# Two pool stacks with waits by tile, and a first cross attention in two streams, three tiles ahead

## The chip, the cores and the metric

The kernel runs on one core of a Trainium2 chip. The metric is the device time of one execution in microseconds. Five engines work side by side, each through its own queue in order: TensorE (PE, with its weight loads shown as PEld), VectorE (DVE), ScalarE (ACT), GpSimd (POOL) and SyncE (SP), which here only issues transfers. They wait for each other through semaphores.

## The reference, cut to what matters

The input x has 16 rows of 128 tokens of 256 numbers; each row is one tile `x[t]` in SBUF. The network has four layers, and each layer is a cross attention to a context of the same size and then a feed-forward part.

- Layer 0: cross attention with 16 heads and quantised products, `h = layernorm(x); x += attend(h, ctx_t)`, which needs only tile t and its context. Then causal self-attention within the tile with 16 query heads and 4 key heads of 128, and a mixture of eight experts, of which two are combined per token (the kernel computes all eight and weights them).
- Layer 1: one-headed cross attention to the tile's context with a mask, then a gated feed-forward part whose three weight matrices are rounded to -1, 0 and 1 by the mean of their absolute values: `s = 1/mean|w|; w_q = clip(round(w*s), -1, 1)/s`. This rounding is part of the computation and is done in the kernel.
- Layer 2: cross attention with 16 heads to the tile's context, then a feed-forward part that picks 4 of 64 small experts.
- Layer 3: cross attention of every tile to the keys and values of all 16 tiles' contexts, then a mixture of ten experts.

Every tile passes the layers in turn; only layer 3's keys and values join the tiles, and those depend on the context alone.

## The kernel before

`run` works in three stages. `l0` (L561) is layer 0; `middle` (L862) is layers 1 and 2 with the keys and values of layer 3; `l3` (L883) is layer 3. Within a stage several streams of tiles stand at different points of the work. Each stream has its own SBUF pool, a pool of small tiles and a tag that names the PSUM banks it uses (`stream`, L116). The work of a tile is a Python generator cut into steps by `yield`, and `side_by_side` (L122) goes through the running generators step by step. A scheduler then orders the instructions of each engine; it may move an instruction ahead of its step, so the steps are only a guide. In `l3` alone the order is the written one.

Layer 0, per tile t:

- `l0_xattn` (L342), the cross attention, starts at step 4t and takes seven steps. Its heads come in four groups (`attention`, L249). Per group POOL spreads the keys (kx, L259), PE makes scores (L262), DVE takes the maximum and subtracts it (L264, L271), ACT the exponential (L272), PE transposes (L209), ACT copies (L225) and PE multiplies with the values (av, L278).
- `l0_keys` (L482) starts at step 4t+8: keys and values of the self-attention.
- `l0_group` (L504) starts at steps 4t+11 to 4t+14, once for each four query heads: projection q, rotation and norm (L464), transposes, scores (L518), softmax on DVE, ACT and POOL (L520 to L527), transposes, oT (L531), and output projection (oproj, L539).
- `l0_moe` (L545) starts at step 4t+17: routing, eight gate-and-up products (gu), and the down product (moe).

The eight PSUM banks of layer 0 are x, av, aq, a, as and ap with one buffer each and m with two. The query tiles of a group go through aq, the scores through as, and everything is transposed through a, so that the groups follow each other in a chain.

SBUF is one stack: a stage's pools are opened over those of the stage before, and every tile of a new pool waits until all of the old pool that it overlaps has been released. `middle` begins with `l1_ffn_weights` (L612). It loads the three raw matrices, sums their absolute values on DVE (L622), multiplies the sums with a matrix of ones on PE (L624), scales and clips on DVE (L631, L632) and converts on ACT (L633). Then come the other weights of the middle, in the order of SP's queue. The expert weights of layer 3 (pool w4) are loaded after the middle.

Of the kernel before, what the change touches and what calls it, by code (L numbers as in the profile page):

```python
# [40 lines left out]
class Net:  # L41
    def __init__(self, tc, pools, ins, out):
        self.tc, self.nc, self.i, self.out = tc, tc.nc, ins, out
        self.const, self.small = pools
        self.small0 = self.small
        self.ps = self.tag = None
        self.setup()
# [66 lines left out]

    @contextmanager
    def stream(self, name, bufs=2, small=3, tag=None):  # L116

        with (self.tc.tile_pool(name=name, bufs=bufs) as pool,
              self.tc.tile_pool(name=f"{name}_s", bufs=small) as sm):
            yield pool, sm, tag or name  # L120

    def side_by_side(self, starts):  # L122


        running, step = [], 0
        while running or any(k >= step for k in starts):
            running += [(st, make(self.enter(st))) for st, make in starts.get(step, ())]
            still = []
            for st, gen in running:
                self.enter(st)  # L130
                try:
                    next(gen)
                    still.append((st, gen))
                except StopIteration:
                    pass
            running, step = still, step + 1
# [12 lines left out]
    @contextmanager  # L149
    def psum(self, **bufs):  # L150

        with self.tc.tile_pool(name="psum", bufs=1, space=PSUM) as self.ps:
            self.bufs = bufs
            yield
            self.ps = None

    def bank(self, shape, tag, name, dtype=F32):
        return self.ps.tile(shape, dtype, name=name, tag=tag, bufs=self.bufs[tag])
# [90 lines left out]
    def attention(self, qT, kT, v, scale, pool, per_row=False):  # L249
# [4 lines left out]
        av = self.bank([P, NH, 17], "av", "av")  # L254

        def group(g):
            oc, hs = g // 2, slice(4 * (g % 2), 4 * (g % 2) + 4)
            kx = pool.tile([P, 4, P], F32, name="kx", tag="kx", bufs=2)
            nc.gpsimd.tensor_tensor(kx, kT[oc].unsqueeze(1).to_broadcast([P, 4, P]),  # L259
                                    self.hmask[:, hs].unsqueeze(2).to_broadcast([P, 4, P]), ALU.mult)  # L260
            ps = self.mm([P, 4, P], "scores")
            nc.tensor.matmul(ps, qT[:, oc, :], kx, start=True, stop=True)  # L262
            mx = self.s(4, "mx")
            nc.vector.tensor_reduce(mx, ps, AX.X, ALU.max, negate=per_row)  # L264
            p = pool.tile([P, 4, P], F32, name="p", tag="p", bufs=3 if per_row else 2)
            if per_row:
                nc.vector.tensor_scalar(mx, mx, scale, None, ALU.mult)  # L267
                for h in range(4):
                    nc.scalar.activation(p[:, h, :], ps[:, h, :], AF.Exp, bias=mx[:, h:h + 1], scale=scale)  # L269
            else:  # L270
                nc.vector.tensor_tensor(p, ps, mx.unsqueeze(2).to_broadcast([P, 4, P]), ALU.subtract)  # L271
                nc.scalar.activation(p, p, AF.Exp, scale=scale)  # L272
            return p

        def product(g, p):
            pT = self.transposed(p.rearrange("p h k -> p (h k)"), 4, pool, "pT", bufs=1 if per_row else 2)
            for h in range(4):
                nc.tensor.matmul(av[:, 4 * g + h, :], pT[:, h, :], v[:, 4 * g + h, :], start=True, stop=True)  # L278
# [52 lines left out]
    def l0_xattn_weights(self):  # L331
        w = {}
        with self.tc.tile_pool(name="l0x_q", bufs=1) as pool:
# [110 lines left out]
    def l0_ffn_weights(self, pool):  # L444
        nc, w = self.nc, {}
        w["q"] = self.load("L0_ffn_qT", [P, 2, 2048], "wa", "(c p) n -> p c n", p=P)
        w["kv"] = self.load("L0_ffn_kvT", [P, 2, 1024], "wc", "(c p) n -> p c n", p=P)
# [13 lines left out]
        w["moe"] = self.moe_weights("L0_ffn", 8)  # L461
# [94 lines left out]
    @contextmanager  # L556
    def l0_weights(self, pool):
        self.tag = "x"
        yield self.l0_xattn_weights(), self.l0_ffn_weights(pool)

    def l0(self):  # L561

        with self.tc.tile_pool(name="l0w", bufs=1) as wp, self.psum(x=1, av=1, aq=1, a=1, **{"as": 1}, ap=1, m=2), self.l0_weights(wp) as (wx, wf), (
                self.stream("x", bufs=1, small=2)) as sx, self.stream("a") as sa, self.stream("m", small=2) as sm:
            tiles = {}

            starts = {}
            for t in range(NT):
                starts.setdefault(4 * t, []).append((sx, lambda p, t=t: self.l0_xattn(t, wx, p)))
                starts.setdefault(4 * t + 8, []).append((sa, lambda p, t=t: self.l0_keys(t, wf, tiles, p)))  # L570
                for g in range(4):
                    starts.setdefault(4 * t + 11 + g, []).append(
                        (sa, lambda p, t=t, g=g: self.l0_group(t, g, wf, tiles, p)))
                starts.setdefault(4 * t + 17, []).append((sm, lambda p, t=t: self.l0_moe(t, wf, tiles, p)))
            self.side_by_side(starts)
        self.tag, self.small = None, self.small0
# [35 lines left out]
    def l1_ffn_weights(self):  # L612

        nc, W = self.nc, self.W1
        w = {"subln": self.rows("L1_ffn_subln_weight", "subln")}
        with self.tc.tile_pool(name="l1r", bufs=1) as pool:
            raw = [self.load("L1_ffn_gateT", [P, 2, W], "ra", "(c p) n -> p c n", p=P, pool=pool),
                   self.load("L1_ffn_upT", [P, 2, W], "rb", "(c p) n -> p c n", p=P, pool=pool),
                   self.load("L1_ffn_downT", [P, 8, D], "rc", "(c p) n -> p c n", p=P, pool=pool)]
            sums = self.s(3, "wsum")  # L620
            for j, r in enumerate(raw):
                nc.vector.tensor_reduce(sums[:, j:j + 1], r, AX.XY, ALU.add, apply_absolute_value=True)  # L622
            ps = self.mm([P, 3], "wtot")
            nc.tensor.matmul(ps, self.ones, sums, start=True, stop=True)  # L624
            mean = w["mean"] = self.w.tile([P, 3], F32, name="wmean", tag="wmean")
            nc.vector.tensor_scalar(mean, ps, 1.0 / (W * D), 1e-5, ALU.mult, ALU.max)
            r = self.s(3, "wr")
            nc.vector.reciprocal(r, mean)
            for j, (n, v) in enumerate(zip(("gate", "up", "down"), raw)):
                w[n] = self.w.tile(list(v.shape), BF16, name=f"tern{j}", tag=f"tern{j}")  # L630
                nc.vector.tensor_scalar(v, v, r[:, j:j + 1], 1.0, ALU.mult, ALU.min)  # L631
                nc.vector.tensor_scalar(v, v, -1.0, MAGIC, ALU.max, ALU.add)  # L632
                nc.scalar.activation(w[n], v, AF.Identity, bias=self.unmagic)  # L633
        return w
# [227 lines left out]
    def middle(self, w3):  # L862

        with (self.tc.tile_pool(name="w1", bufs=1) as self.w, self.psum(e=1, w=3, x=2, av=1, f=1)):
            self.tag = "e"
            w1f = self.l1_ffn_weights()
            w2x, w2f, w3k = self.l2_xattn_weights(), self.l2_ffn_weights(), self.l3_kv_weights()
            with (self.stream("f", bufs=1, small=2) as s2f, self.stream("x", bufs=1, small=2) as s2x,
                  self.stream("kv", bufs=1, small=2, tag="f") as s3, self.stream("f1", bufs=1, small=2, tag="e") as s1f,
                  self.stream("x1", bufs=1, small=2, tag="e") as s1x):  # L870
                starts = {}
                for t in range(NT):
                    for step, st, make in ((0, s1x, lambda p, t=t: self.l1_xattn(t, p)),
                                           (3, s1f, lambda p, t=t: self.l1_ffn(t, w1f, p)),
                                           (7, s2x, lambda p, t=t: self.l2_xattn(t, w2x, p)),
                                           (16, s2f, lambda p, t=t: self.l2_ffn(t, w2f, p)),
                                           (2, s3, lambda p, t=t: self.l3_keys(t, w3k, w3, p))):
                        starts.setdefault(4 * t + step, []).append((st, make))
                starts[4].append((s3, lambda p: self.l3_values(w3k, w3, p)))
                self.side_by_side(starts)  # L880
        self.tag, self.small = None, self.small0

    def l3(self, w3, moe_w):  # L883
# [13 lines left out]
        with (tc.tile_pool(name="l3x", bufs=2) as pool, tc.tile_pool(name="l3p", bufs=3) as pp,  # L897
              tc.tile_pool(name="l3t", bufs=LAG + 1) as tp, tc.tile_pool(name="l3m", bufs=1) as mp,
              tc.tile_pool(name="l3e", bufs=3) as ep):
# [282 lines left out]
    def run(self):  # L1182
        self.load_x()
        with self.tc.tile_pool(name="w0", bufs=1) as self.w:
            self.l0()
        with self.tc.tile_pool(name="w3", bufs=1) as self.w:
            w3 = self.l3_weights()
            self.middle(w3)
            with self.tc.tile_pool(name="w4", bufs=1) as self.w:
# [72 lines left out]
```

## Time and profile before

| what | value |
|---|---|
| median of three runs | 3008.33 us (3003.62 to 3014.27) |
| profiled execution, its own time | 3011.51 us |
| its span, first to last instruction | 3009.8 us |
| PE, DVE, ACT, POOL busy, whole span | 82%, 65%, 58%, 33% |
| layer 0 (first cross attention to last expert product) | 27 to 1154.6 us |
| a tile of layer 0 between 336 and 892 us | 61.8 us |
| layer 1's first readout and first gate product | 1182.1 and 1192.0 us |
| the middle's last output product ends | 1862.5 us |
| layer 3's first exponential | 1877.5 us |

All times within a trace count from the first instruction. A line of a timeline gives the start, the duration, the engine, the line of the kernel, the operation, output and inputs, and in brackets how long the engine was idle before it and what ended that. The profile of the stages gives busy time per engine in a window; as matmuls are pipelined and their ends modelled, busy PE is not always PE at its peak.

### The profile page before, as it was taken

How to read it: one execution, taken by the hardware profiler on the slowest of the kernel's cores; microseconds unless marked ns; L12 is line 12 of the kernel's file. 1: busy time of each engine (PE TensorE's matmuls, PEld its weight loads, DVE VectorE, ACT ScalarE, POOL GpSimd, SP SyncE). 2: the span in 40 equal slices, each digit the busy share in tenths (PEclk: the TensorE clock that was granted, in tenths of full speed). 3: DMA queues.
4: the chain of work that ended last, by engine and by line, in shares of the span. 5: the costliest groups of instructions: out<-in, count | busy, mean ns of one | idle time of the engine just before them, and what ended most of it. 6: DMA issues, size and time to landing. Idle time of an engine off the chain costs nothing. (4 is left out here: it accounts for less than half of the span.)

```text
span 3009.8 us, 41685 instructions
## 1 busy us (share of the span) xinstructions
PE 2460.5 (82%) x14066; PEld 1556.2 (52%) x14066; DVE 1956.3 (65%) x5041; ACT 1755.0 (58%) x4636; POOL 1000.7 (33%) x1587
## 2 busy tenths in 40 slices
PE   4789999999999875888888885777777777777778
PEld 2456666666666543456555653344444444444445
DVE  2455666666665434566666653887788787878784
ACT  1234444444444332555555541998888888888885
POOL 2344444444443322555555541111111111112111
PEclk9899999999999887999999997589899898989999
DMA  5000000000000003000000002876666666666673
GB/s 205 1 1 1 1 1 1 1 1 1 1 1 1 1 28 102 6 3 5 5 5 4 3 1 72 154 135 123 124 117 128 121 124 121 126 122 125 118 128 62
DMA packets 559830, 171.38 MB, mean 57 GB/s; under 512 B 538912, under 2 KB 555904, under 8 KB 558848
## 3 DMA queue, kind: packets, MB, share of 16 engines
q1 hardware_dynamic: 559616, 168.72, 27.8%
q8 instruction: 111, 1.82, 0.2%
q14 instruction: 103, 0.84, 0.1%
HBM read 32.37 MB, written 2.10 MB: 11 GB/s over the span
## 5 line engine op out<-in xcount | busy, mean ns | idle before, releaser
L938 ACT ACTIVATE p<-piece,nb,hs 128x512 int16<-128x512 f32 x1024 | 785.2, 791 | 27.4 <-issue 17.0
L922 DVE TENSOR_REDUCE nm<-piece 128x1 f32<-128x512 f32 x1024 | 652.1, 684 | 107.7 <-PE piece L916 99.8
L916 PE MATMUL piece<-kst,qT 128*128 128x512 bf16 x1024 | 366.5, 414 | 200.6 <-DVE ma L1099 89.6
L1100 POOL TENSOR_TENSOR act<-ma,mb 128x176 f32<-128x176 f32 x160 | 89.0, 558 | 765.1 <-DVE ma L1099 764.7
L233 PE MATMUL gu<-w_L_ffn_wgu,mhT 128*128 128x352 f32 x640 | 252.5, 523 | 11.6 <-ACT p L938 8.0
L225 ACT COPY pT<-tp 128x512 f32<-128x512 f32 (+1 forms) x208 | 116.6, 563 | 201.6 <-PE tp L209 200.1
L916 PEld LDWEIGHTS <-qT 128*128 128x128 bf16 x1024 | 77.4, 99 | 297.2 <-issue 168.8
L938 ACT ACTIVATION_READ_ACCUMULATOR p<-piece,nb,hs 128x1 f32 x1024 | 222.2, 217 | 0.0
L259 POOL TENSOR_TENSOR kx<-kT,hmask 128x512 f32<-128x512 f32 x128 | 132.8, 1043 | 190.4 <-PE scores L262 125.4
L264 DVE TENSOR_REDUCE mx<-scores 128x4 f32<-128x512 f32 x128 | 88.2, 689 | 161.3 <-PE scores L262 161.0
L233 PEld LDWEIGHTS gu<-w_L_ffn_wgu,mhT 128*128 128x128 f32 x640 | 122.7, 205 | 131.4 <-ACT p L938 83.5
L950 PEld LDWEIGHTS <-pT 128*128 128x128 f16 x4096 | 144.7, 99 | 82.6 <-issue 68.0
L278 PEld LDWEIGHTS av<-v,pT 128*128 128x128 f32 x1024 | 136.2, 201 | 78.2 <-ACT pT L225 66.6
L233 PE MATMUL gu<-w_L_ffn_wgu,hT 128*128 128x352 f32 x512 | 173.7, 461 | 2.1 <-DVE act L432 1.6
L524 ACT ACTIVATE s<-s,nb,qs 128x128 f32<-128x128 f32 x256 | 123.2, 482 | 87.2 <-DVE nb L522 87.2
L278 PE MATMUL av<-v,pT 128*128 128x17 f32 x1024 | 136.3, 265 | 41.0 <-ACT pT L225 41.0
L269 ACT ACTIVATE p<-scores,mx,qs 128x128 f32<-128x128 f32 x256 | 96.9, 459 | 118.8 <-DVE mx L267 111.0
L950 PE MATMUL av<-v_int,pT 128*128 128x16 bf16 x4096 | 143.7, 171 | 19.6 <-DVE o L1021 19.6
L262 PE MATMUL scores<-kx,qT 128*128 128x512 f32 x256 | 153.0, 682 | 2.3 <-ACT qT L225 1.8
L539 PE MATMUL oproj<-w_L_ffn_oT,oT 128*128 128x256 f32 x512 | 128.9, 396 | 3.7 <-ACT oT L533 3.6
L1119 PE MATMUL moe<-w_L_ffn_wd,aT 128*128 128x256 f32 x448 | 127.7, 434 | 3.6 <-ACT p L938 3.6
L233 PE MATMUL q<-w_L_ffn_qT,hT 128*128 128x512 f32 x256 | 127.9, 600 | 2.1 <-DVE rot L478 2.0
(362 smaller groups left out, 5305.7 us busy)
## 6 DMA issues: line engine op xcount, KB each, us to landing
pT<-p SPq DMA_TRANSPOSE x256, 4.3
w_L_ffn_wgu<-in_L_ffn_wgu SPq DMA_DIRECT2D x1, 3520.0 KB, 11.6
w_L_ffn_wgu<-in_L_ffn_wgu SPq DMA_DIRECT2D x1, 2816.0 KB, 12.7
x<-in_x SPq DMA_DIRECT2D x16, 128.0 KB, 4.5
ctxT<-in_ctxT SPq DMA_DIRECT2D x4, 512.0 KB, 5.2
w_L_ffn_qT<-in_L_ffn_qT SPq DMA_DIRECT2D x1, 2048.0 KB, 7.9
w_L_ffn_oT<-in_L_ffn_oT SPq DMA_DIRECT2D x1, 2048.0 KB, 15.6
ctx<-in_ctx SPq DMA_DIRECT2D x16, 128.0 KB, 2.0
```

What stands on the lines that cost most here:

```text
L225: nc.scalar.copy(out[:, j0:j0 + m, :], ps)
L233: self.nc.tensor.matmul(ps, a, b, start=(j == 0), stop=(j == n - 1))
L259: nc.gpsimd.tensor_tensor(kx, kT[oc].unsqueeze(1).to_broadcast([P, 4, P]), self.hmask[:, hs].unsqueeze(2).to_broadcast([P, 4, P]), ALU.mult)
L262: nc.tensor.matmul(ps, qT[:, oc, :], kx, start=True, stop=True)
L278: nc.tensor.matmul(av[:, 4 * g + h, :], pT[:, h, :], v[:, 4 * g + h, :], start=True, stop=True)
L524: nc.scalar.activation(s[:, j, :], s[:, j, :], AF.Exp, bias=nb[:, j:j + 1], scale=qs[:, j:j + 1], accum_out=z[:, j:j + 1])
L539: nc.tensor.matmul(proj, oT[:, j, :], w["o"][:, c, :], start=(c == 0), stop=(c == 15))
L916: nc.tensor.matmul(ps, qTs[t % 2][:, hd, :], kst[q // 2][:, hd // 2, 512 * (q % 2):512 * (q % 2) + 512], start=True, stop=True)
L922: nc.vector.tensor_reduce(st["nm", u][:, q:q + 1], st["s", u, q][0], AX.X, ALU.max, negate=True)
L938: nc.scalar.activation(p[:, 512 * q:512 * q + 512], ps, AF.Exp, bias=nb, scale=st["sq", t][:, hd:hd + 1], accum_out=st["z", t][:, hd, q:q ...
L950: nc.tensor.matmul(st["av", t][:, hd, :], pb[:, c, :], v[:, c, hd * 16:(hd + 1) * 16], start=(c == 0), stop=(c == NT - 1))
L1119: nc.tensor.matmul(ps, st["aT", k][:r, j, :], wd[:r, c, :], start=(c == 0), stop=(c == 13))
```

## The change

All SBUF and PSUM pools are now opened with waits by tile: a tile waits only for those old tiles whose bytes it takes. SBUF becomes two stacks, one from the left and one from the right end. On the left stand the weights and the stream of layer 0's self-attention, its expert weights and, from step 17, the expert stream; on the right stand the cross attention's weights and streams. The weights of layer 1 (`w1`) and the layer 1 streams of the middle follow on the right, and the weights of the middle (`w2`) and the layer 2 streams on the left.

Layer 0's cross attention runs in two streams at first. Tiles 1, 3 and 5 use a second stream `y`, with the banks of the expert stream (m0 for its products, m1 for av) and single buffers; tiles 0, 2 and 4 use stream `x`. Tile t starts at step 2t up to tile 5 and at 4(t-3) after that, so that from tile 6 on the cross attention is three tiles further ahead. Stream y is closed before the experts begin.

`l1_ffn_weights` becomes a generator, `prepare`, that starts at step 60 of layer 0, once the cross attention is over; it has two raw buffers instead of three, sums and converts one matrix after the other, and uses bank x. In the built program its DVE passes stand among the work of tiles 10 and 11. In layer 0's loads the keys' weights come before the query weights.

```diff
+    def pool(self, name, bufs, side="left"):
+        return self.tc.tile_pool(name=name, bufs=bufs, side=side, reuse_waits="tile")
...
-    def side_by_side(self, starts):
+    def side_by_side(self, starts, hooks={}):
         running, step = [], 0
         while running or any(k >= step for k in starts):
+            if step in hooks:
+                hooks[step]()
...
-        with self.tc.tile_pool(name="psum", bufs=1, space=PSUM) as self.ps:
+        with self.tc.tile_pool(name="psum", bufs=1, space=PSUM, reuse_waits="tile") as self.ps:
...
     def bank(self, shape, tag, name, dtype=F32):
+        if tag == "m":
+            self.turns += 1
+            tag = ("m0", "m1")[self.turns % 2]
...
-        av = self.bank([P, NH, 17], "av", "av")
+        twice = 1 if self.tag == "m0" else 2
+        av = self.bank([P, NH, 17], "m1" if self.tag == "m0" else "av", "av")
...
-            kx = pool.tile([P, 4, P], F32, name="kx", tag="kx", bufs=2)
+            kx = pool.tile([P, 4, P], F32, name="kx", tag="kx", bufs=twice)
...
+        w["kv"] = self.load("L0_ffn_kvT", [P, 2, 1024], "wc", "(c p) n -> p c n", p=P)
         w["q"] = self.load("L0_ffn_qT", [P, 2, 2048], "wa", "(c p) n -> p c n", p=P)
-        w["kv"] = self.load("L0_ffn_kvT", [P, 2, 1024], "wc", "(c p) n -> p c n", p=P)
...
+    def l0(self, late):
+        early = ExitStack()
         self.tag = "x"
+        with self.psum(x=1, av=1, aq=1, a=1, **{"as": 1}, ap=1, m0=1, m1=1):
+            self.w = early.enter_context(self.pool("wx", 1, "right"))
+            wx = self.l0_xattn_weights()
+            sx = early.enter_context(self.stream("x", bufs=1, small=2, side="right"))
+            with (self.pool("wa", 1) as self.w, self.stream("a") as sa, self.pool("wm", 1) as wm,
+                  ExitStack() as third):
+                wf = self.l0_ffn_weights(self.w)
+                self.w = wm
+                wf["moe"] = self.moe_weights("L0_ffn", 8)
+                self.tiles(wx, wf, sx, sa, early, late, third)
...
+    def tiles(self, wx, wf, sx, sa, early, late, third):
+        ahead, BEGIN = ExitStack(), 17
+        sy, sm = ahead.enter_context(self.stream("y", bufs=1, small=2, tag="m0", side="right")), []
+        def begin():
+            ahead.close()
+            sm.extend(third.enter_context(self.stream("m", small=2)))
+        hooks[BEGIN] = begin
+        def prepare(pool):
+            early.close()
+            self.w = late.enter_context(self.pool("w1", 1, "right"))
+            yield from self.l1_ffn_weights()
             for t in range(NT):
-                starts.setdefault(4 * t, []).append((sx, lambda p, t=t: self.l0_xattn(t, wx, p)))
+            other = t in (1, 3, 5)
+            step = 2 * t if t < 6 else 4 * (t - 3)
+            starts.setdefault(step, []).append((sy if other else sx, lambda p, t=t: self.l0_xattn(t, wx, p)))
...
+        starts.setdefault(4 * NT - 4, []).append((sa, prepare))
+        self.side_by_side(starts, hooks)
...
-            sums = self.s(3, "wsum")
-            for j, r in enumerate(raw):
-                nc.vector.tensor_reduce(sums[:, j:j + 1], r, AX.XY, ALU.add, apply_absolute_value=True)
+            for j, (n, shape) in enumerate(shapes.items()):
+                yield
+                if j == 2:
+                    raw[n] = self.load(f"L1_ffn_{n}T", shape, "raw0", "(c p) n -> p c n", p=P, pool=pool)
+                v, total, r = raw[n], self.s(1, "wsum"), self.s(1, "wr")
+                nc.vector.tensor_reduce(total, v, AX.XY, ALU.add, apply_absolute_value=True)
+                ps = self.bank([P, 1], "x", "wtot")
...
-        with (self.tc.tile_pool(name="w1", bufs=1) as self.w, self.psum(e=1, w=3, x=2, av=1, f=1)):
-            w1f = self.l1_ffn_weights()
+        w1f = self.w1f
+        with (self.psum(e=1, w=3, x=2, av=1, f=1), self.stream("x1", bufs=1, small=2, tag="e", side="right") as s1x,
+              self.stream("f1", bufs=1, small=2, tag="e", side="right") as s1f, self.pool("w2", 1) as self.w,
+              self.stream("kv", bufs=1, small=2, tag="f") as s3, self.stream("x", bufs=1, small=2) as s2x,
+              self.stream("f", bufs=1, small=2) as s2f):
...
-            with self.tc.tile_pool(name="w4", bufs=1) as self.w:
+            late.close()
+            with self.pool("w4", 1, "right") as self.w:
```

## The prediction

> **What bounds the kernel now.** I read first the busy time by stage, because the change touches only some stages. Columns: window, its length, then busy time (instructions) of PE, PEld, DVE, ACT and POOL, granted clock, DMA share, GB/s.
>
> ```profile
> 27.00:86.00 59.00, 35.88 (x100) 20.37 (x100) 19.16 (x52) 7.37 (x17) 19.83 (x36) 1.00 0.36 124
> 86.00:140.00 54.00, 39.99 (x138) 22.77 (x138) 22.65 (x54) 14.71 (x32) 20.25 (x30) 0.78 0.00 0
> 140.00:211.00 71.00, 59.91 (x272) 39.09 (x271) 36.85 (x86) 29.21 (x77) 33.44 (x46) 0.90 0.00 1
> ...
> 336.00:892.00 556.00, 524.23 (x2547) 359.74 (x2546) 342.55 (x918) 255.24 (x702) 255.03 (x363) 1.00 0.00 1
> ...
> 954.00:1017.00 63.00, 54.10 (x210) 35.02 (x209) 29.78 (x87) 23.91 (x68) 23.43 (x33) 0.86 0.00 1
> 1017.00:1075.00 58.00, 50.91 (x211) 32.80 (x210) 28.07 (x75) 23.45 (x67) 20.71 (x30) 0.97 0.00 1
> ...
> 1154.50:1192.00 37.50, 12.50 (x33) 5.81 (x33) 18.16 (x49) 8.84 (x11) 11.16 (x25) 0.61 0.56 174
> ...
> 1820.00:1863.00 43.00, 20.57 (x66) 13.93 (x66) 13.71 (x29) 3.91 (x7) 9.63 (x10) 0.72 0.00 0
> ```
>
> From 336 to 892 PE is busy 94%: nine tiles in 556 us, 61.8 us a tile, bound by PE. Only three places have slack: the ramp (27 to 211), the last tiles of layer 0, which have no cross attention beside them (954 to 1075), and the two seams (1154 to 1192, 1820 to 1863). At the first seam PE works 12.5 of 37.5 us. Its timeline says why:
>
> ```profile
> 1154.62 0.37 SPq L95 DMA_DIRECT2D w_L_xattn_Wq<-in_L_xattn_Wq  x1
> ...
> 1165.79 3.75 PE L233 MATMUL kv<-w_L_xattn_kvT,ctxT 128*128 128x512 f32 x4 [6.82 <-DMA w_L_xattn_oT<-in_L_xattn_oT]
> ...
> 1176.93 2.08 PE L233 MATMUL k<-w_L_xattn_Wkv,ctxT 128*128 128x256 f32 x4 [7.39 <-DMA w_L_xattn_Wkv<-in_L_xattn_Wkv]
> ...
> 1182.06 1.22 PE L607 MATMUL read<-ctx,pT 128*128 128x256 f32 x2 [0.35 <-ACT pT L225]
> ...
> 1191.95 1.06 PE L233 MATMUL gate<-tern,hT 128*128 128x512 bf16 x2
> ```
>
> The last expert product of layer 0 ends at 1154.59. Only then does the first weight of the middle leave SP's queue, since its pool waits for the whole of layer 0; PE waits for those bytes twice.
>
> Last, single rows of the ramp. The same two matmuls of 512 columns take 2.07 us there and 1.10 in a dense stage:
>
> ```profile
> 36.93 2.07 PE L262 MATMUL scores<-kx,qT 128*128 128x512 f32 x2 [0.46 <-ACT qT L225]
> ...
> 44.69 2.05 PE L262 MATMUL scores<-kx,qT 128*128 128x512 f32 x2
> ```
> ```profile
> 1800.38 1.10 PE L262 MATMUL scores<-kx,qT 128*128 128x512 f32 x2
> ```
>
> PE runs at half speed in the ramp (the clock column's 1.00 from 27 to 86 is not borne out by these durations, which decide).
>
> **Part 1: first seam, gain.** In the changed build the middle's weights take bytes 101,664 to 138,608 of a partition. Those held layer 0's attention stream (99,136 to 139,460), not the expert weights (from 139,488). The attention stream's last tile is read by the residual add that ends at 1120.5 and the normalisation that ends at 1121.8. Before, the loads took from 1154.6 to 1176.9, 22.3 us; begun at 1121.8 they land by 1144, ten microseconds before PE needs them. Layer 1's ternary weights are loaded and rounded earlier still, in layer 0. What remains after the last expert product, with the cold rows of the trace in the new PE order: transpose 0.5, key projection 2.1 beside the copy 0.4, scores 0.7, the four kv matmuls 3.7 (softmax, 1.2, lies under them), transpose and copy 0.8: the readout starts 7.9 us after the product, where it started 27.5 after (1182.06 less 1154.59). From there to the gate matmul 9.9 us stay. Gain 19.6, some 22 if PE stays at full speed, 16 if the loads are up to 4 us late. I take 20.
>
> Before the seam, in the last tile's experts, DVE's third sum over raw weights (2.28 us from 1136.87) keeps the next expert waiting until 1139.07 although its ACT result stood at 1137.34. That sum moves away: gain 1.7.
>
> **Part 2: second seam, next to nothing.** PE's order is unchanged there: layer 3's first transpose stands behind the last output matmul of the middle in both builds, and the chain before it (x add, routes, z, transposes, output) is untouched. The zeroing of the two query buffers on POOL (1.80 each) moves from ahead of a power that the last tile waits for (delayed from about 1822.6 to 1824.4, partly under DVE's routes) to the place after z, under 6 us of output matmuls. Gain 1 (0 to 2). Layer 3's expert weights may load sooner, but are first used some 30 units into layer 3.
>
> **Part 3: cross attention two tiles abreast, three ahead.** A tile of it costs PE 12.8 us: its rows between 700 and 762 sum to 15.1 of 69.2, scaled to the 58.5 us that PE was busy. Three tiles, 38 us, move from the steady stage into the ramp, where PE is idle 23, 14 and 11 us of the first three windows: 48. With everything hidden the ramp grows by nothing; with nothing hidden, by 38, or more with PE at half speed. In between stands a chain: one group of a tile takes 7.75 us (36.93 to 44.69), 5.1 of it PE. Two groups in the new order share PE: transposes 1.1, wait for the copy 1.3, products 1.9, scores 2.06, twice: 12.8 at half speed. At full speed 0.6, 1.3, 1.0, 1.1 makes 8.0 for two.
>
> Which of them is a matter of the clock. Row: PE's longest run in the old ramp is 3.8 us (products and scores), then 3.7 idle, and it stayed slow. Rule: the Trainium skill, "TensorE: Matmul & The Clock Gate", section "What's actually happening", has PE doubled in speed after a window of about 3.4 us sustained work, and halved after such a window idle. The new runs (products, scores, next transposes) are 5.1 us and the waits 1.3, so the rule says full speed after a round or two: the ramp then grows by about 6 us. By the old rows alone it grows by some 30: four rounds at 12.8 for 7.75 are 20, and another 9 or so until the third tile. I take 6, range -8 to 30.
>
> The same rule speaks against the other end. Layer 0's last tiles lose their cross attention: five tiles instead of two run without it. That should save 12.8 a tile, but the two that did took 63 and 58 us (the projections start at 954, 1017 and 1075), not 49: the chain of each group sets the pace, and PE falls idle long enough to slow down:
>
> ```profile
> 994.06 1.11 PE L209 MATMUL tp<-ident,s 128*128 128x128 f32 x4 [3.70 <-POOL s L527]
> ...
> 998.59 3.78 PE L539 MATMUL oproj<-w_L_ffn_oT,oT 128*128 128x256 f32 x8 [0.68 <-ACT oT L533]
> ```
>
> (Eight of those take 1.89 elsewhere.) Three more such tiles at 60.7 for 61.8 save 3; at 58, 11; at 63 they lose 4. I take 3.
>
> **Part 4: layer 1's weights inside layer 0, cost.** Three sums of 2.28, six passes of 1.2 to 1.3 (14.3 us of DVE) and three ACT passes of 2.0 now stand in the queues of tiles about 10 and 11, with softmax steps of a group behind them on both engines; PE waits for those. The passes had been on idle engines; the cover is DVE's idle half (28 of 58 us busy). One row warns:
>
> ```profile
> 1163.43 1.21 DVE L632 TENSOR_SCALAR w_L_ffn_downT<-w_L_ffn_downT 128x2048 f32<-128x2048 f32 x1
> ...
> 1163.57 1.48 POOL L178 TENSOR_TENSOR ln_r<-rp,mhalf 128x1 f32<-128x1 f32 x1
> ```
>
> POOL's power takes 0.55 elsewhere, so a DVE pass can hold POOL, which ends each group's softmax. The third load also waits until ACT has freed the first raw buffer (1 MB, 5 to 10 us to land), and DVE's queue waits with it. All twelve hidden costs 0; half of each in the way, 10. I take 4 (0 to 12). SP's added waits hold back nothing else in layer 0, which issues no other transfer then; two mask loads wait for POOL's casts of tiles 0 and 1, which also lie in layer 0, ahead of the middle's weights. At the start the expert weights (2.8 MB) now go before the keys' weights, about 10 us later for these; they are needed near 86, forty microseconds after.
>
> **Sum.** +6 - 3 + 4 - 1.7 - 20 - 1 = -15.7. On the span of 3009.8: 2994; the profiled run's time is 1.7 above its span, 2996, and stands 3.2 above the median of the runs: 3008.3 - 15.7 = 2992.6. I say 2993.
>
> **Rivals.** (a) The seam's gain stands and the rest nets to nothing or little: 2977 to 2999, likeliest. (b) The ramp and the weight passes eat it: ramp +15, passes +8, late tiles 0: 3008 - 20 - 2.7 + 23 = 3008. For it: PE's 94% means that moved work is not removed work. Within 0.3% of 3008.3 (9 us, about what a measurement of this kernel can tell from no change), 2999 to 3017. (c) Slower: PE stays at half speed through the two-stream ramp. Ramp +32, late tiles +4, passes +8, against 22.7: 3030. It decides once the ramp grows by more than about 31 with the other terms as taken. Against it: the 5.1 us runs. (d) More gain: the ramp runs dense enough to gain the half-speed stretches back (-8), late tiles at 58 (-11), seam 22: 2968. (e) The pools change nothing, because some tile of the middle still sits on late bytes: the seam stays, and +5 remains: 3013. The byte addresses speak against it; it is counted in (b).
>
> **Chances.** (a) 0.47, (b) with (e) 0.22, (c) 0.14, (d) 0.17. Faster 0.64, same 0.22, slower 0.14. The range reaches from (d)'s near half to past (b): 2966 to 3020; (a)'s own is 2977 to 2999.
>
> **What would show it.** Right: PE's gap after the last expert product under 3 us, the readout 6 to 9 us behind it; SP issuing the middle's weights some 30 us before that product; score pairs of 1.1 us by the third round of the ramp; the last five tiles of layer 0 near 60 us each. Wrong: score pairs still at 2.07 us beyond 80 us; POOL's softmax products delayed around the weight passes; layer 0 ending more than 20 us later than before.

## The result, and the profile after

The changed kernel takes 2985.96 us, median of five runs (2978.52 to 2997.94), beside 3008.33 for the kernel before: ratio 0.9927, 95% interval 0.9898 to 0.9956, 22.4 us less. Its profiled execution took 2981.85 us with a span of 2980.1, at a mean granted clock of 0.922. The profiled execution before shows 0.922 too, but has no clock record ahead of 91 us, and by its rows PE ran at half speed there from 27 us on; counted so, its mean is about 0.91 (an estimate). The two profiled executions lie 29.7 us apart, 7.3 more than the medians: one was 3.2 us slower than its kernel's median, the other 4.1 faster. The stages below add up to the 29.7.

The stages after, in the columns of the stage table of before (window, length, busy time and instructions of PE, PEld, DVE, ACT and POOL, granted clock, DMA share, GB/s):

```profile
27.00:86.00 59.00, 43.60 (x208) 27.97 (x207) 32.24 (x74) 15.65 (x34) 26.54 (x43) 0.86 0.36 130
86.00:140.00 54.00, 46.71 (x217) 30.31 (x218) 30.80 (x76) 19.07 (x43) 26.03 (x36) 0.87 0.00 1
140.00:211.00 71.00, 63.59 (x313) 42.94 (x312) 42.87 (x104) 31.79 (x82) 35.31 (x49) 0.93 0.00 1
338.50:892.00 553.50, 507.63 (x2368) 343.34 (x2367) 336.19 (x878) 247.89 (x672) 235.92 (x341) 0.98 0.02 8
962.50:1022.60 60.10, 51.41 (x207) 32.88 (x206) 27.47 (x76) 23.70 (x67) 20.42 (x29) 0.91 0.00 1
1022.60:1081.00 58.40, 51.32 (x213) 32.74 (x212) 29.00 (x79) 23.67 (x66) 21.16 (x31) 0.97 0.02 5
1158.80:1174.00 15.20, 7.75 (x31) 4.26 (x30) 7.86 (x30) 3.03 (x8) 7.23 (x14) 0.72 0.04 10
1795.00:1837.00 42.00, 21.13 (x66) 14.52 (x66) 12.04 (x27) 3.91 (x7) 9.60 (x10) 0.67 0.21 82
```

The first three windows hold more PE work than before (153.9 us for 135.8), as meant. In the fourth the granted clock is 0.98 where it was 1.00, and the layer is no shorter: its last expert product ends at 1158.8, before at 1154.6. The seam is another matter: 15.1 us from that product to the first gate product, where it was 37.4. Its timeline, SP's queue first, then PE:

```profile
1041.40 0.38 SPq L96 DMA_DIRECT2D w_L_xattn_qT<-in_L_xattn_qT  x1
...
1086.66 0.46 SPq L96 DMA_DIRECT2D w_L_xattn_Wq<-in_L_xattn_Wq  x1
...
1127.44 0.37 SPq L96 DMA_DIRECT2D w_L_xattn_Wkv<-in_L_xattn_Wkv  x1
```
```profile
1153.80 5.02 PE L243 MATMUL moe<-w_L_ffn_wd,actT 128*128 128x256 f32 x22 [0.56 <-DVE actT L237]
1158.65 0.38 PE L219 MATMUL tp<-ident,ln_h 128*128 128x128 f32 x2
1158.87 1.03 PE L243 MATMUL k<-w_L_xattn_Wkv,ctxT 128*128 128x256 f32 x4
...
1162.58 0.70 PE L644 MATMUL read<-ctx,pT 128*128 128x256 f32 x2 [0.35 <-ACT pT L235]
1169.48 1.01 PE L827 MATMUL htp<-identb,parts 128*128 128x128 bf16 x8 [6.21 <-DVE qs L251]
...
1173.89 0.63 PE L243 MATMUL gate<-tern_gate,hT 128*128 128x512 bf16 x1 [0.22 <-issue]
```

The weights leave 117 to 31 us ahead of the product's end and PE goes on without a gap, the key projection at full speed (1.03 us; cold 2.08). The readout stands 3.8 us behind the product, before 27.5.

In the ramp the pairs of score matmuls reach 1.10 us in the third round of the changed kernel, where the first five of the kernel before, up to 80.8 us, took 2.05 to 2.07:

```profile
34.84 1.38 PE L273 MATMUL scores<-kx,qT 128*128 128x512 f32 x2 [0.46 <-ACT qT L235]
37.11 2.04 PE L273 MATMUL scores<-kx,qT 128*128 128x512 f32 x2 [0.46 <-ACT qT L235]
41.18 1.10 PE L273 MATMUL scores<-kx,qT 128*128 128x512 f32 x2
```

Full speed holds up to 62 us and comes and goes afterwards; one pair, at 89.8 us, still takes 2.05.

### The profile page after: what moved, and what is told of

It reads as the page before. It is cut to its first block, busy times and chain, and to the rows that moved or that the text cites. A ratio compares the mean times of both kernels' runs of the same rounds, so it can differ in the third digit from the quotient of the medians.

```text
span 2980.1 us, 41711 instructions
## 1 busy us (share of the span) xinstructions
PE 2448.5 (82%) x14053; PEld 1548.8 (52%) x14070; DVE 1958.2 (66%) x5045; ACT 1756.6 (59%) x4636; POOL 997.9 (33%) x1587
## 5 line engine op out<-in xcount | busy, mean ns | idle before, releaser
L243 PE MATMUL gu<-w_L_ffn_wgu,mhT 128*128 128x352 f32 x640 | 254.7, 527 | 11.6 <-ACT p L976 7.9
L549 PEld LDWEIGHTS oproj<-w_L_ffn_oT,oT 128*128 128x128 f32 x512 | 100.3, 203 | 53.1 <-ACT oT L543 34.2
```

The source lines that it names most:

```text
L243: self.nc.tensor.matmul(ps, a, b, start=(j == 0), stop=(j == n - 1))
L549: nc.tensor.matmul(proj, oT[:, j, :], w["o"][:, c, :], start=(c == 0), stop=(c == 15))
```

## The experiments

The stages of every kernel's profiled execution, in us; tile 3, 10 and 15 mean the start of that tile's first output projection. The last column counts the stretches of 3.4 us in layer 0 that the trace's clock records show at half speed. Where the cross attention has one stream up to tile 3 (before, one stream, its repeat, its fill, four left out), these records begin only at 90 to 91 us, so that the slow ramp, some 19 stretches, is missing from that column.

| kernel | start to tile 3 | 3 to 10 | 10 to 15 | 15 to last product | layer 0 ends | seam to gate | middle | second seam | layer 3 | half-speed |
|---|---|---|---|---|---|---|---|---|---|---|
| before | 336.0 | 432.8 | 306.8 | 79.0 | 1154.6 | 37.4 | 670.5 | 14.9 | 1132.3 | 25 |
| changed | 338.5 | 436.6 | 305.9 | 77.8 | 1158.8 | 15.1 | 663.3 | 14.6 | 1128.3 | 39 |
| changed, again | 338.2 | 436.7 | 309.1 | 77.8 | 1161.9 | 15.1 | 663.3 | 14.6 | 1129.6 | 39 |
| waits by pool | 344.2 | 437.2 | 308.9 | 77.8 | 1168.1 | 15.8 | 666.1 | 20.3 | 1132.2 | 44 |
| pools exchanged | 341.6 | 436.7 | 309.3 | 77.9 | 1165.4 | 9.7 | 685.7 | 14.6 | 1130.6 | 45 |
| one stream | 331.4 | 432.7 | 308.7 | 80.2 | 1152.9 | 15.1 | 665.7 | 14.6 | 1130.9 | 24 |
| before + streams | 339.0 | 436.6 | 306.0 | 79.3 | 1161.0 | 39.3 | 671.9 | 14.9 | 1127.9 | 42 |
| two streams in the ramp only | 326.8 | 432.3 | 310.7 | 80.3 | 1150.0 | 14.7 | 666.2 | 14.6 | 1122.7 | 37 |
| no passes | 335.2 | 437.1 | 308.9 | 77.8 | 1159.0 | 14.7 | 663.8 | 14.6 | 1128.2 | 42 |
| four left out | 331.6 | 441.0 | 312.7 | 77.7 | 1162.9 | 14.6 | 672.9 | 14.6 | 1131.2 | 45 |
| ramp only, again | 336.3 | 436.1 | 311.9 | 77.7 | 1162.0 | 14.7 | 670.6 | 14.6 | 1131.1 | 39 |
| ramp only, with fill | 337.5 | 434.6 | 308.4 | 74.6 | 1155.1 | 14.7 | 670.4 | 14.6 | 1128.0 | 33 |
| one stream, again | 335.9 | 432.7 | 310.0 | 77.8 | 1156.4 | 15.1 | 663.3 | 14.6 | 1129.4 | 25 |
| one stream, with fill | 335.5 | 432.7 | 305.2 | 77.1 | 1150.4 | 15.1 | 665.6 | 14.6 | 1126.3 | 21 |

Theory S: the gain is the first seam's, and the cross attention in two streams and three tiles ahead brings nothing. Theory W: the waits by tile bring it. Theory X: the streams bring part of it.

**The changed kernel again**, without an edit.

> The changed kernel once more, unaltered, to tell what belongs to the program from what differs between executions. If the stages are the program's: every mark within 0.5 us of the first profile (layer 0 ends at 1158.8, first to last readout of layer 1 547.2, layer 3's first exponential to the end 1128.3), and the two gains that no step of the sum contains, 5.7 us in the middle and 4.1 in layer 3, stay. If they are chance of one execution: the marks move by several us, towards 552.9 and 1132.4.

2987.99 us (2985.51 to 2996.28), ratio 0.9939, 0.9920 to 0.9958. Middle and second seam came out to the tenth; layer 3 moved by 1.3 and layer 0 by 3.1, all of it in tile 10 (66.5 us where it was 63.3). Two other kernels that were profiled twice moved more: one stream ran the middle in 665.7 and 663.3 us, two streams in the ramp only ran it in 666.2 and 670.6 and layer 3 in 1122.7 and 1131.1. So a difference of 3 us in a stage of a single profile proves nothing, nor does one of some 8 us in layer 3, and the agreement to the tenth does not make the shorter middle the program's.

**Waits by pool.**

```diff
-        return self.tc.tile_pool(name=name, bufs=bufs, side=side, reuse_waits="tile")
+        return self.tc.tile_pool(name=name, bufs=bufs, side=side, reuse_waits="pool")
```
(and the same for the PSUM pool)

> The changed kernel with every wait by pool instead of by tile; the order of instructions on each engine is the same. Theory S (the seam's gain comes from which bytes the middle's weights lie on: those of the attention stream, which is done some 33 us before the last expert product): the loads are issued from about 1122 instead of 1041 on, land by about 1145, the readout starts 4 to 6 us behind the last product, and the time is within 3 us of the changed kernel's 2986. Theory W (the waits by tile bring it): the loads leave only behind the last product, the readout is some 20 us later again, and the time is about 3006.

2995.62 us (2985.97 to 3009.24), ratio 0.9959, 0.9942 to 0.9975. At the first seam theory S holds: the loads are issued from 1136.74 (expected 1122), 31 us ahead of the last product at 1168.1, and the readout follows 4.5 us behind it. The median is 7.6 above the changed kernel on the same chip, not within 3, but the two intervals overlap. The profiled executions are 18.0 apart; 6.0 of that stand in the ramp, where another kernel differs by more between two executions (326.8 and 336.3), and 5.7 at the second seam, 20.3 instead of 14.6, which all other kernels with two stacks cross in 14.6. DVE's rows there, and POOL's:

```profile
1849.95 0.42 DVE L808 TENSOR_TENSOR x<-out,x 128x256 f32<-128x256 f32 x1 [12.09 <-PE out L243]
1854.60 0.41 DVE L1003 TENSOR_SCALAR ln_h<-x,ln_mv,ln_r 128x256 f32<-128x256 f32 x1 [4.23 <-POOL ln_r L188]
...
1850.06 0.12 POOL L1181 MEMSET act<- 128x32 f32 x1 [10.11 <-PE out L243]
1850.12 3.54 POOL L1183 MEMSET qT<- 128x2048 bf16 x2
...
1854.01 0.56 POOL L188 TENSOR_TENSOR ln_r<-rp,mhalf 128x1 f32<-128x1 f32 x1
```

With waits by pool POOL's zeroing for layer 3 waits for the middle's last output product, and the power behind it in POOL's queue waits too; in the changed kernel the zeroing stands right behind z and is over when the output products begin at 1830.94:

```profile
1827.19 0.12 POOL L1181 MEMSET act<- 128x32 f32 x1
1827.26 3.54 POOL L1183 MEMSET qT<- 128x2048 bf16 x2
```

So the waits by tile pay at the second seam, not at the first.

**Two pools of the left stack exchanged.**

```diff
-            with (self.pool("wa", 1) as self.w, self.stream("a") as sa, self.pool("wm", 1) as wm,
+            with (self.pool("wa", 1) as self.w, self.pool("wm", 1) as wm, self.stream("a") as sa,
```

> The changed kernel with two pools of the left stack exchanged: the expert weights lie under the attention stream, so that the middle's weights take the expert weights' bytes; waits stay by tile, everything before the seam as it is. Theory S (place of the bytes): layer 1's first readout starts 12 to 24 us later behind the last expert product than the 3.8 us of the changed kernel, and the time rises by 10 to 20 us, to 2996 to 3006. Theory W (waits by tile are enough wherever the bytes lie) or theory X (the cross attention's streams, not the seam, bring the gain): the readout stays within 5 us of that product, and the time within 5 us of 2986.

3003.62 us (2993.39 to 3011.21), ratio 0.9986, 0.9974 to 0.9999: 15.6 above the changed kernel on the same chip. The loads are late again, as theory S says:

```profile
1157.62 0.38 SPq L96 DMA_DIRECT2D w_L_xattn_qT<-in_L_xattn_qT  x1
...
1168.41 0.37 SPq L96 DMA_DIRECT2D w_L_xattn_Wkv<-in_L_xattn_Wkv  x1
```

The readout is not late, though (3.3 us behind the product): the scheduler put layer 3's key projection further back. The loss came out in the middle's first tiles (the third readout stands 72.5 us behind the product instead of 63.6, the seventh 230.3 instead of 214.4), where PE has nothing beside layer 1's chain:

```profile
1187.73 0.88 PE L219 MATMUL tp<-ident,a 128*128 128x128 f32 x3 [9.43 <-DVE a L708]
```

The middle takes 685.7 us instead of 663.3, against 5.4 won to the gate: 17.0 net from the last product to the middle's end. The place of the bytes decides when the loads leave, and most of the gain rests on it. Since the edit also changed the scheduler's order, what late loads cost by themselves is not separated. Of the 29.5 us that the changed kernel gains over that stretch (707.9 before, 678.4 changed) 12.5 remained; whether they come from the earlier preparation of layer 1's weights or from the order was not tested.

**Cross attention in one stream.**

```diff
-            other = t in (1, 3, 5)
-            step = 2 * t if t < 6 else 4 * (t - 3)
+            other, step = False, 4 * t
...
-        starts.setdefault(4 * NT - 4, []).append((sa, prepare))
+        starts.setdefault(4 * NT + 8, []).append((sa, prepare))
```

> The changed kernel with layer 0's cross attention back in one stream, tile t at step 4t, and layer 1's weights prepared from step 72 (behind the cross attention of the last tile) instead of 60. Theory S (the streams bring nothing or cost a little): the ramp is 2.5 us shorter, the full tiles come back to 61.8 us from 62.4 (3.8 us), layer 0 ends at 1153 to 1156 instead of 1158.8, the seam keeps its gain (readout 4 to 8 us behind the last product), and the time is 2980 to 2984. Theory X (the streams bring part of the gain): layer 0 ends at 1162 or later, and the time is 2990 or more.

2978.00 us (2975.87 to 2981.01), ratio 0.9899, 0.9880 to 0.9919; the changed kernel on the same chip 2988.0 (2985.5 to 2996.3), with no overlap. Theory X falls: without the streams the kernel is not slower, and 10 us faster on this chip. Layer 0 ends at 1152.9, its full tiles are back at 61.8 us, and the seam is the same. The edit also moves the preparation of layer 1's weights, but the tiles from 3 to 10, which lie ahead of it in both kernels, take 432.7 us instead of 436.7: these 4 us belong to the streams. The profiled executions differ by only 5.2, so the rest of the 10 is not placed.

**The streams alone, on the kernel before.**

```diff
-                starts.setdefault(4 * t, []).append((sx, lambda p, t=t: self.l0_xattn(t, wx, p)))
+                step = 2 * t if t < 6 else 4 * (t - 3)
+                starts.setdefault(step, []).append((sy if t in (1, 3, 5) else sx, lambda p, t=t: self.l0_xattn(t, wx, p)))
```
(with stream y, its banks and its closing at step 17 as in the change)

> The kernel before with part 3 of the change alone: cross attention in two streams until the experts begin, three tiles ahead afterwards; pools, waits and layer 1's weights as before. Theory S (the streams bring nothing): the ramp grows by 2 to 6 us, the tiles from 336 to 760 us take 62.0 to 62.4 us instead of 61.8, layer 0 ends at 1157 to 1163 instead of 1154.6, the first seam stays at 27 us, and the time is 3010 to 3017. Theory X (the streams bring part of the gain): layer 0 ends before 1150 and the time is below 3003.

3021.63 us (3016.78 to 3025.83), ratio 1.0059, 1.0037 to 1.0080: slower. The stages agree with theory S (layer 0 ends 6.4 us later), but the profiled execution explains only 5.3 of the 16 us; it was the fastest of its four runs, and where the others lost more is not shown.

**Two streams in the ramp only.**

```diff
-            step = 2 * t if t < 6 else 4 * (t - 3)
+            step = 2 * t if t < 6 else 4 * t
```
(and layer 1's weights from step 72)

> The changed kernel with two streams for tiles 0 to 5 as it has them, but from tile 6 on one stream at step 4t, so no longer three tiles ahead; layer 1's weights from step 72. If being three ahead is what makes the full tiles 62.4 us: from tile 7 on they take 61.8 again, layer 0 ends at 1153 to 1157, and the time is 2978 to 2983, like the single stream's 2978. If the ramp in two streams is the costly part: layer 0 ends at 1158 to 1163 and the time stays at 2985 to 2990. The tiles between 3 and 6, now without cross attention beside them, take 60 to 62 us if a tile without it is no faster, 49 to 55 if PE sets its pace.

2973.20 us (2969.87 to 2975.45), ratio 0.9895, 0.9876 to 0.9914. From tile 7 on a tile takes 61.8 us again: being three ahead is what makes 62.4. The three from tile 3 to 6, mostly without cross attention, take 61.8, 61.1 and 58.3, and the next 65.6.

**Without layer 1's passes.**

```diff
-                nc.vector.tensor_reduce(total, v, AX.XY, ALU.add, apply_absolute_value=True)
...
-                nc.scalar.activation(w[n], v, AF.Identity, bias=self.unmagic)
+                nc.vector.memset(w[n], 0.0)
+                nc.vector.memset(mean[:, j:j + 1], 1.0)
```

> The changed kernel with the sums, scaling, clipping and conversion of layer 1's weights left out of layer 0 (the three weight matrices and their means are set to constants, three short fills each for nine DVE passes and three of ACT); the loads stay. Part 4 as predicted (the passes cost 4 us, between 0 and 12): the five tiles from 775 to 1081 us take 300 to 304 us instead of 306 to 309, and layer 0 ends some 4 us sooner. If they are wholly hidden: 306 to 309 as in the changed kernel. If they also slow PE's clock: 295 to 299, and 8 to 12 us off the time.

Tiles 10 to 15 take 308.9 us, as in the changed kernel: the passes look hidden. But tile 11 was slow here, 63.4 us for 61.2 in the changed kernel. The streams on the kernel before give a better comparison, since there layer 1's passes come after layer 0: tile 10 took 63.6 us and the five tiles 306.0. With the passes tile 10 took 66.4 to 66.8 in three of four executions and the five tiles 308.9 to 309.3; the fourth is the first profile of the changed kernel (63.3 and 305.9). So about 3 us are likely. The time, 2979.57 us (2972.41 to 2981.97), ratio 0.9906 with 0.9884 to 0.9928, has an interval that overlaps the changed kernel's, so nothing is settled by it. What stands in the changed kernel's trace is PE waiting for a sum:

```profile
810.10 1.94 PE L243 MATMUL gu<-w_L_ffn_wgu,hT 128*128 128x352 f32 x6
816.08 0.38 PE L667 MATMUL wtot<-wsum,ones 128*128 128x1 f32 x2 [4.03 <-DVE wsum L665]
817.28 1.12 PE L219 MATMUL tp<-ident,s 128*128 128x128 f32 x4 [0.82 <-POOL s L537]
819.07 2.08 PE L541 MATMUL oT<-pT,v 128*128 128x512 f32 x2 [0.68 <-ACT pT L235]
```

The third raw load is issued at 808.51, when ACT has freed the buffer, the sum ends at 816.02, and PE, in order, stands still with all that is queued behind; then it runs at half speed (2.08 us for a pair that takes 1.02 at full). The 4.0 us are not all a cost: the transposes next in the queue need the softmax, which POOL finished only at 817.23.

**Four cross attentions left out.**

```diff
-            starts.setdefault(step, []).append((sy if other else sx, lambda p, t=t: self.l0_xattn(t, wx, p)))
+            if t not in (8, 9, 10, 11):
+                starts.setdefault(step, []).append((sy if other else sx, lambda p, t=t: self.l0_xattn(t, wx, p)))
```
(on the one-stream kernel)

> The single-stream kernel with layer 0's cross attention of tiles 8 to 11 left out altogether, in the middle of the dense stage, to measure what four times 12.8 us of PE work are worth there. If PE's work sets the pace of a tile: four tiles at about 49 us, layer 0 ends some 50 us sooner, at 1102. By the step of the prediction (a light tile takes 60.7 us, 58 to 63): 4 to 15 us sooner, 1138 to 1149. If the group's chain and PE's clock give all of it back: within 4 us of 1152.9.

Some 51 us of PE work less, and layer 0 ended at 1162.9, 10 us later than in the first profile of the kernel that does it and 6.5 later than in a second one (below). This kernel ran once. None of the three expectations had that sign. From the start of tile 5 (455) the one-stream kernel's four tiles take 247.2 us, this one's 256.5. The same stretch in both, first with the cross attention, then without:

```profile
455.00:702.20 247.20, 233.15 (x1133) 159.98 (x1132) 152.68 (x411) 113.59 (x313) 114.15 (x165) 1.00 0.00 1
```
```profile
454.90:702.20 247.30, 221.07 (x938) 149.10 (x938) 128.00 (x344) 99.26 (x276) 97.48 (x141) 0.92 0.00 1
```

In the same time PE issues 195 matmuls fewer and is busy only 12 us less, since its clock falls to 0.92. The groups' chain (softmax on DVE, ACT and POOL) has nothing beside it to fill PE's waits; PE falls below a share of work, and everything on it takes twice as long for 3.4 us and more.

**Work that nobody uses.** If that is so, useless work should help.

> The kernel with two streams in the ramp alone once more, unaltered, as the base of the next run on the same chip: layer 0's last tile from its first output projection to the last expert product 80.3 us, with nine half-speed stretches of 3.4 us between 1094 and 1128; time 2970 to 2977.

> The same kernel with work added that nobody uses: behind the score matmuls of the last tile's third and fourth query group, five matmuls of 512 columns each into the free bank x, some 5.5 us of PE work at full speed, where PE waits for softmax and nothing else is left to do. Theory C (PE's clock follows its share of work in the 3.4 us before): the nine half-speed stretches between 1094 and 1128 fall to four or fewer, the last tile takes 70 to 76 us instead of 80.3, and the time falls by 4 to 10 us. If the waits themselves are what costs, the added matmuls stand in the way or change nothing: 80 to 86 us for the last tile, and the time the same or up to 6 us longer.

```diff
+        if t == 15 and g > 1:
+            fill = self.bank([P, 4, P], "x", "fill")
+            for _ in range(5):
+                nc.tensor.matmul(fill, self.ident, qT, start=True, stop=True)
```

The base came to 2980.50 us (2979.31 to 2994.65), ratio 0.9903, on a chip where the streams in the ramp gained nothing, and its profiled execution was the slowest of its five; its last tile took 77.7 us with six half-speed stretches, not 80.3 with nine. With the fill (8.9 us of PE work) it took 74.6 with two. PE's order in the base and with the fill, from the fourth group on:

```profile
1113.56 1.16 PE L528 MATMUL scores<-kT,qT 128*128 128x128 f32 x8 [0.68 <-ACT qT L235]
1120.02 1.12 PE L219 MATMUL tp<-ident,s 128*128 128x128 f32 x4 [5.31 <-POOL s L537]
1121.81 2.07 PE L541 MATMUL oT<-pT,v 128*128 128x512 f32 x2 [0.68 <-ACT pT L235]
1124.56 3.49 PE L549 MATMUL oproj<-w_L_ffn_oT,oT 128*128 128x256 f32 x8 [0.68 <-ACT oT L543]
```
```profile
1110.17 1.05 PE L530 MATMUL scores<-kT,qT 128*128 128x128 f32 x8
1111.06 4.46 PE L535 MATMUL fill<-qT,ident 128*128 128x512 f32 x10
1116.98 0.66 PE L219 MATMUL tp<-ident,s 128*128 128x128 f32 x4 [1.47 <-POOL s L543]
1118.31 1.12 PE L547 MATMUL oT<-pT,v 128*128 128x512 f32 x2 [0.68 <-ACT pT L235]
1120.11 1.99 PE L555 MATMUL oproj<-w_L_ffn_oT,oT 128*128 128x256 f32 x8 [0.68 <-ACT oT L549]
```

Idle or filled, PE waits for the same softmax, 6.5 and 6.8 us from the scores to the transposes; filled, it then runs at full speed. The whole time did not move: 2981.27 us (2978.45 to 2984.55), ratio 0.9905. The fill also moved the third weight product: it stood in tile 13, at 1001.0, and now stands in the last tile, at 1102.8, and tile 13 took 63.1 us instead of 66.6. So the fill was tried on the one-stream kernel too:

> The single-stream kernel once more, unaltered, as the base of the next run: 2976 to 2981; layer 0 ends at 1152 to 1154, the last tile from its first output projection to the last expert product takes 80.2 us.

> The single-stream kernel with the same ten unused matmuls behind the score matmuls of the last tile's third and fourth query group. Theory C (PE's clock follows its share of work): the last tile takes 74 to 76 us instead of 80.2, with two or three half-speed stretches instead of nine, layer 0 ends near 1148, and the time falls by about 5 us, to 2972 to 2976. If the fill only takes the place of waits: 78 us or more, and no change of the time.

2980.46 us (2976.28 to 2984.13) without and 2976.04 (2973.71 to 2979.31) with the fill; ratios 0.9918 (0.9901 to 0.9936) and 0.9905 (0.9888 to 0.9922), which overlap: 4 us that are likely and not settled. The last tile went from 77.8 to 77.1 only, with five half-speed stretches instead of six; the expected 74 to 76 did not come. Tile 13 went from 66.4 to 62.8, because the scheduler again placed the third weight product in the last tile, where its sum was long ready. So having that product where its sum is late costs about 3.5 us in both kernels.

The fastest versions here take 2973 to 2981 us: one stream 2976 to 2980, two streams in the ramp only 2973 on one chip and 2981 on another, which doesn't set the two apart.

## Why the prediction was right

**First seam (-20).** Right in mechanism and nearly in size: -22.3 to the gate (37.4 to 15.1). The readout stands 3.8 us behind the product, not 7.9, because PE stayed at full speed, the 22 of the range; of it 1.4 went back between readout and gate. That the loads leave early because of the bytes they take is shown by the exchange of the pools, which also gave back 15.6 us of the time; how much of the gain the loads bring alone, and how much the order and the earlier preparation, is not separated. The working started the loads at 1121.8; by tile they started at 1041, and it made no difference, as the kernel with waits by pool shows.

**Second seam (-1).** -0.3. But the step had no price for the other side: under two stacks with waits by pool the seam would have cost 5.4 us more than before. The waits by tile prevent that loss.

**Ramp (+6).** Right. Five profiled executions with one stream there reach tile 3 at 331.4 to 336.0, mean 334.1; six with the changed kernel's starts at 335.2 to 344.2, mean 339.5: +5.4. The two profiles compared first differ by only 2.5, and single ones scatter by more than 4. With two streams but no tiles ahead tile 3 comes at 326.8 to 337.5: the streams alone cost nothing, the work moved into the ramp does. The rule of the Trainium skill weighed there, "TensorE: Matmul & The Clock Gate", section "What's actually happening", decided well against the old rows: full speed came between the first and the sixth score pair and stayed for several rounds. The sign named against it, pairs at 2.07 us beyond 80, showed in single pairs (2.05 at 89.8).

**Light tiles (-3) and weight passes (+4).** Together +1 was taken for tiles 10 to 15; -0.9 and +2.3 were measured. Taken apart, the streams on the kernel before give -0.8 for the light tiles, and three of four executions put the passes at some 3 us above that. The reason given for expecting 60.7 us and not 49 (each group's chain sets the pace, and PE's clock falls) was right and stronger than the step had it: leaving the work out altogether made tiles slower in the one execution of that kernel, and a light tile saved next to nothing. Of the passes, the chain named (third load behind ACT's pass, then the sum) came as written, with PE waiting 4.0 us. Whether a pass would hold POOL's power stayed untested, since none of the powers ran beside a pass in the changed kernel. POOL's products that began just ahead of a pass kept their 1.27 us, and the pass behind one took 1.58 us instead of 1.23.

**DVE's third sum (-1.7).** -1.2 in the last tile, which is within what one kernel shows there in two executions (80.2 and 77.8 with one stream).

**What the sum lacked.** The tiles between 3 and 10 were taken as unchanged and grew by 3.8 us, as moving the cross attention three tiles ahead changed PE's order there; this is the program's, since all six executions with those starts show it (436.6 to 437.2). And from the gate to the end 11.6 us went between the two profiled executions (7.2 in the middle, 4.0 in layer 3, 0.3 at the second seam), for which the sum has 1. Much of that is the clock again: from the gate to the eighth readout 7 half-speed stretches touch the middle instead of 12, and layer 3 has 65 instead of 71; other kernels with an unchanged layer 3 ran it in 1122.7 with 62 and in 1131.2 with 72. But the same program differs as much from one execution to the next (layer 3 in 1122.7 and 1131.1), and one stream, with the same first seam, had 11 of those stretches in its first profile and 7 in its second. So a gain in layer 3 is not shown. The middle averages 666.5 us over the ten executions with early loads and waits by tile, where the two with late loads have 670.6 and 671.9; a gain of some 4 us there is likely and its cause is open.

So rival (a) is what happened: the seam's gain stands and the rest nets to little. -15.7 was forecast, -22.4 and -20.6 were measured in two sets of runs. With the terms as measured the sum is about -16: ramp +5.4, tiles 3 to 10 +3.8, light tiles -0.8, passes +3, last tile -1.2, first seam -22.3, second seam -0.3, middle -4. The two missing terms cancel in it, which is luck. The 4 to 6 us that are left over lie within what single profiles scatter by.

## What to carry to other kernels

At a stage's seam ask on which old bytes the next stage's first weights will lie: putting them on the buffers that are done first was worth some 16 us of the time here, and finer waits did nothing more for it. Work taken out of a stage where PE is 94% busy bought nothing here, since the rest is a chain of small waits; look at the granted clock of what remains before counting the saved time. A product on PE that waits for another engine's pass belongs behind the point where its input is surely ready, since all of PE's queue stands behind it.

## What the runs showed of the hardware

In every trace PE's clock changes only on a fixed grid of 3.413 us, which agrees with the Trainium skill, "TensorE: Matmul & The Clock Gate", section "What's actually happening" (a window of that length that doesn't restart with the kernel). The section speaks of an idle window before the clock falls and one window of sustained work before it doubles. Counted over the fourteen profiled executions, from the first clock record of each, with PE's busy share in a stretch and the clock of the next:

| PE busy in a stretch | at full speed: next one at half | at half speed: next one at half |
|---|---|---|
| under 0.4 | 373 of 373 | 136 of 136 |
| 0.4 to 0.5 | 243 of 261 | 18 of 18 |
| 0.5 to 0.6 | 285 of 561 | 37 of 37 |
| 0.6 to 0.7 | 132 of 767 | 154 of 154 |
| 0.7 to 0.8 | 9 of 2169 | 193 of 207 |
| 0.8 to 0.9 | 0 of 1363 | 306 of 404 |
| over 0.9 | 0 of 4595 | 78 of 1002 |

No idle stretch is needed: a busy share of 0.6 can lose full speed, and getting it back took a share above 0.9 in most cases. (Busy ends are modelled, so the shares are those of the profile.) It costs the changed kernel's dense stage two stretches in seven tiles. This wait of 1.34 us fell into a stretch with a share of 0.61:

```profile
515.15 0.41 PE L219 MATMUL tp<-ident,hn 128*128 128x128 f32 x2 [1.34 <-DVE hn L499]
```
```profile
L243 PE MATMUL k<-w_L_ffn_kvT,hT 128*128 128x512 f32 x4 | 3.3, 981 | 0.0
```

The key projection behind it took 981 ns a matmul, 592 in the kernel before, where the same wait is 1.08 us and no stretch between 262 and 992 us is at half speed.
